# A four-layer sparse graph network: scoring one block ahead, and the order of a layer's last blocks

## The chip, the cores and the metric

The kernel runs on one core of a Trainium2 chip. The metric is the device time of one execution in microseconds (us), as a median over runs. A core has five engines that work through instruction queues of their own and wait for one another by semaphores: TensorE (PE: matrix products into the accumulation memory PSUM), VectorE (DVE: elementwise work and reductions), ScalarE (ACT: activation functions and copies), GpSimd (POOL: here it issues indirect DMAs) and SyncE (SP: here it issues plain DMAs).

## The reference, cut to what matters

The input is `x`, 4096 nodes with 256 features, and a sparse symmetric adjacency matrix `adj`. Four layers follow one another. Each normalizes the rows, clips them at zero, computes attention over each node's neighbours, and adds the result to `x`:

```
h = maximum(layernorm(x), 0);  x = x + L0(h, adj)   # 4 heads, leaky_relu 0.2, elu
h = maximum(layernorm(x), 0);  x = x + L1(h, adj)   # 1 head, leaky_relu 0.01, Wh + att @ h
h = maximum(layernorm(x), 0);  x = x + L2(adj, h)   # 4 heads, leaky_relu 0.2, biases
h = maximum(layernorm(x), 0);  x = x + L3(h, adj)   # q, k, v with 4 heads
# in each: e = score(i, j) for neighbours j;  alpha = softmax(e over j)
#          out_i = sum_j alpha_ij * value_j
```

A node's score against a neighbour is, in layers 0 to 2, a sum of two numbers, one from each node's row, and in layer 3 a product of query and key. So a layer needs, for each node, the rows of all its neighbours as the layer before left them.

## The kernel before

**Lists.** The first part (up to about 360 us in the profile) reads `adj`, finds each node's neighbours and sorts the nodes by their number of neighbours. The sorted nodes form 32 blocks of 128, one node per partition. `CAPS` gives the neighbour slots of a block: block 0 has 23 (15 of them, `KEPT`, are gathered for all its nodes, the others are shared in one more gather), then 14, 13, and so on down to 3 in block 31.

**A layer.** `layer(l)` runs layers 1 to 3 over the blocks in the order `ORDER`: 0, 30, 1, 29, 2, 28 and so on to 14, 16, 15, 31. The last five blocks are thus 17 (8 slots), 14 (9), 16 (8), 15 (8) and 31 (3); 18 (8 slots) and 13 (9) come ahead of them. `nt` is 32, `i` counts through `ORDER`, and `left` is `nt - 1 - i`. For every slot of a block, GpSimd issues one indirect DMA (`fetch`, L1048) that gathers 128 rows of the layer's table `tab[l]` in DRAM into the ring `s_ring`, 36 x 512 floats in each partition; a row has 288 floats in layer 1, 264 in layer 2 and 512 in layer 3. `fill(i)` issues the gathers of up to `AHEAD` = 4 blocks in advance, as far as ring slots are free. A layer's first gather needs every row of its table, so it waits until the layer before has written its last block.

**The steps of a block**, in layers 1 and 2:

- `scores`: VectorE and ScalarE compute the scores `e` from the gathered rows (L1554, L1565 and what follows in layer 2; in layer 1 L1550 and L1551 on ScalarE, and `mutual`, L1608 and L1612, on VectorE), the maximum (L1592, L1596), and ScalarE the exponentials (L1594, L1600).
- `weigh`, the products: VectorE makes the shares (L1626 to L1628) and multiplies the gathered rows by them in the ring (L1654), and TensorE sums the rows by products with the identity (L1662, the last one L1668) into one of three banks `s_acc`.
- `settle`: VectorE reduces the sum into `x` (L1689) and takes mean and variance (L960, L962); ScalarE works out the norm's factors in eight small instructions (L965 to L972) that `normed` issues together with the statistics.
- `norm`: ScalarE normalizes and clips (`s_h`, L975), and TensorE transposes it (L985).
- `flip`: ScalarE copies the transposed block out of PSUM (`s_ht`, L987).
- `product`: TensorE multiplies it with the next layer's weights (L1028). For layer 3 these are two products: keys and values (512 columns) and queries (256 columns).
- `third`, the row read-out: the new rows leave PSUM and go to the next layer's table. In layer 1 ScalarE copies 264 columns (L1710) and SyncE writes them (L1712). In layer 2 VectorE adds the biases, `s_kv` (L1728) and the query (L1732), SyncE writes keys and values (L1730), VectorE multiplies query and key (L1735, L1739), and ScalarE sums squares (two of L1742). `s_kv` has three buffers.

**What sets the order.** The order on PE, DVE, ACT and SP is the order in which the Python code issues instructions (`manual_schedule`); in layers 1 and 2 that holds for POOL too. `layer` keeps counters: `upto("norm", i - N)` brings the step `norm` up to the block at place `i - N`. So `S`, `N`, `F`, `Q` and `T` say how many places the steps `settle`, `norm`, `flip`, `product` and `third` stay behind; they shrink towards the layer's end. In the middle of layers 1 and 2 they are 2, 3, 4, 5 and 6. In each turn of the loop the block's scores and products stand directly behind one another:

```
            upto("norm", i - N)
            upto("product", i - Q)
            ...
            p = self.scores(l, b, self.rows[b], g)
            ...
            sums[b] = self.weigh(l, b, vs.pop(b) if l == 3 else self.rows[b][:, 0:D], g, p)
            ...
            upto("settle", i - S)
            if l < 3:
                upto("flip", i - F)
                upto("third", i - T)
```

`told_by` lets a read of PSUM wait for the last sum (L1668) of the turn in which it was written, if that turn is over. `now` is the turn's number, and `signals` holds those last sums.

Of the kernel before, what the change touches and what calls it, by code (L numbers as in the profile page):

```python
# [20 lines left out]
D = 256  # L21
# [52 lines left out]
RAW = 6  # L74

AHEAD = 4

BOUND = 4900.0


class Sparse:
# [874 lines left out]
    def normed(self, pool, xt, name):  # L956

        nc, act = self.nc, self.nc.scalar.activation
        st = pool.tile([P, 6], F32, name=f"s_st_{name}", tag="st", bufs=3)
        nc.vector.bn_stats(st, xt)  # L960
        mv = pool.tile([P, 2], F32, name=f"s_mv_{name}", tag="mv1", bufs=3)
        nc.vector.bn_aggr(mv, st)  # L962
        y = pool.tile([P, 6], F32, name=f"s_y_{name}", tag="y1", bufs=3)
        log, root, less, minus, r, at = (y[:, k : k + 1] for k in range(6))
        act(log, mv[:, 1:2], AF.Ln, bias=self.eps)  # L965
        act(less, mv[:, 1:2], AF.Identity, bias=self.minus, scale=-0.5)
        act(root, log, AF.Exp, scale=-0.5)
        act(minus, mv[:, 0:1], AF.Copy, scale=-1.0)
        act(log, root, AF.Square)
        act(less, less, AF.Identity, bias=self.three, scale=log)  # L970
        act(r, less, AF.Copy, scale=root)
        act(at, minus, AF.Copy, scale=r)  # L972
        yield None
        h = pool.tile([P, D], F32, name=f"s_h_{name}", tag="h", bufs=2)
        act(h, xt, AF.Relu, bias=at, scale=r)  # L975
        yield h
# [372 lines left out]
    def layer(self, l):  # L1349
# [89 lines left out]
        def settle(c):  # L1439
            behind[c] = self.settle(l, c, sums.pop(c), made)  # L1440
            for _ in range(2):
                next(behind[c])

        def room(k):
            if len(self.free) < k:
                upto("flip", done["norm"] - 1)
                upto("third", done["product"] - 1)
# [26 lines left out]
        def third(d):  # L1474
            if l < 3:
                step, wrote = when["row", d]
                self.reads = []
                next(rows.pop(d), None)
                if step < now:
                    for i in self.reads:  # L1480
                        told_by(i, wrote, step)
            while made and (len(made) > 1 or todo == []):
                i = self.send(*made.pop(0)).ins
                next_in_line(i)
                self.tc.declare_no_dep(i, group="results", reason="places differ")
                self.tc.add_to_no_dep_group("results", i)

        stages = {"settle": settle, "norm": norm, "flip": flip, "product": product, "third": third}
        done = {name: 0 for name in stages}

        def upto(name, k):
# [1 line left out]
                stages[name](ORDER[done[name]])  # L1493
                done[name] += 1

        for i in range(nt):
            now = i
            left = nt - 1 - i
            if l == 3:
                S = 1 if left < 3 else 2  # L1500
                N = F = Q = S + 1
                T = N
            else:
                S = 1 if left < 5 else 2
                N = 2 if left < 4 else 3
                Q = 2 if left < 2 else 3 if left < 4 else 4 if left < 6 else 5
                F, T = max(N, Q - 1), Q + 1
            fill(i)
            if (l, i) == (2, 4):
                self.symmetric()  # L1510
            b = ORDER[i]
            upto("norm", i - N)
            upto("product", i - Q)
            g = ring[:, held[b][0] : held[b][1], :]
            p = self.scores(l, b, self.rows[b], g)
            if l == 3:
                upto("third", i - T)
            sums[b] = self.weigh(l, b, vs.pop(b) if l == 3 else self.rows[b][:, 0:D], g, p)
            start, end = held.pop(b)
            past.append((start * wide, end * wide, self.read))  # L1520
            self.ever.append((start * wide, end * wide, self.read[0]))
            if l < 3:
                signals[i] = self.read[1]
            upto("settle", i - S)
            if l < 3:
                upto("flip", i - F)
                upto("third", i - T)
        now = nt
        upto("norm", nt - 2)
        upto("third", nt - 3)  # L1530
        upto("product", nt - 2)
        upto("settle", nt - 1)
        upto("norm", nt - 1)
        upto("third", nt - 2)
        upto("product", nt - 1)
        upto("third", nt - 1)

    def scores(self, l, b, mine, g):

# [48 lines left out]
        by_head = e[:, : K + 1, :].rearrange("p k h -> p h k")  # L1588
        top = pool.tile([P, H], F32, name=f"s_m_{l}_{b}", tag="m", bufs=3)
        p = self.shares[:, ts(self.turns % 2, TOPK * H)].rearrange("p (k h) -> p k h", h=H)  # L1590
        if l == 1:
            nc.vector.tensor_reduce(top, by_head, AX.X, ALU.max, negate=True)  # L1592
            tot = pool.tile([P, H], F32, name=f"s_t_{l}_{b}", tag="t", bufs=3)
# [21 lines left out]
    def weigh(self, l, b, me, g, made):  # L1615
# [12 lines left out]
        nc.vector.tensor_tensor(  # L1628
            whole(p), whole(exps), tot.unsqueeze(2).to_broadcast([P, H, K + 1]), ALU.mult
        )  # L1630
        self.turns += 1
        v0 = 0 if l < 3 else D
        acc = self.pacc.tile([P, 2, D], F32, tag="acc", name=f"s_acc_{l}_{b}")
        self.took_x[b] = nc.tensor.matmul(  # L1634
# [60 lines left out]
    def advance(self, l, b, ht, made):  # L1695
# [17 lines left out]
        else:  # L1713
# [17 lines left out]
            q = mine[:, 0:D]  # L1731
            i = nc.vector.tensor_tensor(q, ps_q, self.bqkv[:, 0:D], ALU.add)  # L1732
            self.reads.append(i.ins)
            qk = pool.tile([P, 4, 64], F32, name=f"s_qk_{b}", tag="qk", bufs=2)
            nc.vector.tensor_tensor(  # L1735
                qk, q.rearrange("p (h d) -> p h d", h=4),
# [584 lines left out]
```

## Time and profile before

| | |
|---|---|
| median of 3 runs | 1674.33 us (1669.05 to 1676.06) |
| the profiled execution's own time | 1670.3 us |
| its span in the profile | 1668.5 us |
| mean granted TensorE clock | 0.831 |
| layer 1, first gather to last | 539.5 to 875.9 us |
| layer 2, first gather to last | 902.7 to 1240.2 us |
| layer 3, first gather | 1275.2 us |

Times in a profile are microseconds from the span's start, engines are named as above (PEld is TensorE's loading of weights), and L1654 is line 1654 of the kernel before. A group's line gives the line of code, the engine and operation, what it writes and reads, the count, the busy time, the mean of one in ns, and the idle time of the engine ahead of it with what ended that. A line of the timeline gives start, duration, engine, line, operation, and in brackets the idle time ahead of it and its releaser. A line of the waits gives the waiting instruction, what it waited for, the total in us, how often, and the longest.

### The profile page before, as it was taken

The page shows a single profiled execution, that of the slowest core. Times are in us where ns is not written, and L with a number is a line of the kernel's source. Part 1 is how long each engine was busy: PE and PEld are TensorE (multiplying, and loading weights), DVE is VectorE, ACT ScalarE, POOL GpSimd, SP SyncE. Part 2 cuts the span into 40 slices and gives each one's busy share as a digit, 9 for nine tenths or more (in the row PEclk, how much of TensorE's full clock was granted, in tenths as well). Part 3 has the DMA queues.
Part 4 walks back from the last instruction along what each step waited for, and adds up shares of the span by engine and source line. Part 5 has one row for each costly group of instructions (what it writes and reads, how often), then busy time and mean ns, then how long its engine had stood idle before and what let it go on. Part 6 is the DMA issues. An engine that isn't in the chain of part 4 may idle for free.

```text
span 1668.5 us, 14028 instructions
## 1 busy us (share of the span) xinstructions
PE 1074.4 (64%) x3166; PEld 583.3 (35%) x3179; DVE 1108.8 (66%) x2651; ACT 536.1 (32%) x1754; POOL 1142.3 (68%) x1241
## 2 busy tenths in 40 slices
PE   5858888605775367787773567777793455546465
PEld 4513333203443234444442234444352232323232
DVE  5669899816885255555552456777774897888786
ACT  6966664103354033343342023333342000000000
POOL 1267777767774777777772777777753777777775
PEclk9969899857898678788897689999997677877777
DMA  7899999466552444444452445444543777767674
GB/s 267 298 395 394 365 394 331 147 222 162 155 166 69 119 120 127 132 131 134 131 137 65 108 111 148 133 139 133 142 123 106 210 220 205 213 206 211 201 209 132
DMA packets 125908, 309.07 MB, mean 185 GB/s; under 512 B 35028, under 2 KB 53463, under 8 KB 125816
## 3 DMA queue, kind: packets, MB, share of 16 engines
q0 software_dynamic: 66832, 203.64, 42.5%
q1 hardware_dynamic: 58984, 104.46, 17.8%
q8 instruction: 27, 0.44, 0.1%
q14 instruction: 65, 0.53, 0.1%
HBM read 273.00 MB, written 35.00 MB: 185 GB/s over the span
## 4 chain that ended last, share of the span: by engine, by line
POOL 25%; DVE 22%; DMA 20%; issue 15%; ACT 8%; PE 8%; DVEq 0%; POOLq 0%; ACTq 0%; SPq 0%
POOL s_ring L1048 20%; DMA s_ring<-s_tab,s_near 12%; DMA s_raw<-in_adj_dram 6%; DVE s_ring L1654 5%; POOL s_g L1048 2%; DMA s_g<-s_tab,s_keep 2%; POOL s_placed L722 2%; DVE s_ring L1575 1%; ACT s_low L277 1%; PE s_acc L1272 1%; PE s_acc L1662 1%; PE s_bank L1028 1%; DVE s_e L1579 1%; PE s_ps_t L1028 1%; POOL out_dram L1065 1%
## 5 line engine op out<-in xcount | busy, mean ns | idle before, releaser
L1048 POOL DMA_INDIRECT s_ring<-s_tab,s_near x900 | 855.9, 951 | 338.0 <-issue 264.8
L1662 PE MATMUL s_acc<-s_ring,s_ident 128*128 128x512 f32 (+1 forms) x1002 | 459.8, 616 | 275.6 <-DVE s_ring L1654 275.1
L1662 PEld LDWEIGHTS s_acc<-s_ring,s_ident 128*128 128x128 f32 x1002 | 222.2, 229 | 489.7 <-DVE s_ring L1654 305.2
L1048 POOL DMA_INDIRECT s_g<-s_tab,s_keep x192 | 182.8, 952 | 128.5 <-DMA s_raw<-in_adj_dram 66.1
L1654 DVE TENSOR_TENSOR s_ring<-s_ring,s_shares 128x2048 f32<-128x2048 f32 (+1 forms) x153 | 232.9, 1552 | 0.0
L277 ACT ACTIVATE s_low<-s_raw 128x1024 fp8e4<-128x1024 int32 x128 | 135.0, 1055 | 58.6 <-DMA s_raw<-in_adj_dram 56.8
L1600 ACT ACTIVATE s_shares<-s_e 128x40 f32<-128x40 f32 (+7 forms) x64 | 13.1, 205 | 332.7 <-DVE s_e L1597 332.7
L520 PE MATMUL s_pt<-s_low,s_mark_True 128*128 128x512 fp8e4 x256 | 83.9, 408 | 53.2 <-DVE s_cand L532 46.6
L1575 DVE TENSOR_TENSOR s_ring<-s_ring,s_shares 128x2048 f32<-128x2048 f32 (+7 forms) x47 | 78.8, 1676 | 56.4 <-DMA s_ring<-s_tab,s_near 36.4
L965 ACT ACTIVATE s_y<-s_mv,s_eps 128x1 f32<-128x1 f32 x64 | 18.8, 294 | 276.4 <-DVE s_mv L962 250.4
L532 DVE MAX8 s_cand<-s_pt 128x8 f32<-128x256 f32 x256 | 93.1, 416 | 13.8 <-PE s_pt L530 12.3
L1608 DVE TENSOR_SCALAR s_eq<-s_ring,s_own_f 128x207 bf16<-128x207 f32 (+12 forms) x32 | 12.6, 393 | 134.0 <-DMA s_ring<-s_tab,s_near 133.6
L631 PE MATMUL s_ae<-s_g,s_ident 128*128 128x512 f32 x192 | 93.0, 614 | 3.0 <-DVE s_g L622 2.9
L1579 DVE TENSOR_REDUCE s_e<-s_ring 128x32 f32<-128x2048 f32 (+7 forms) x47 | 78.9, 1679 | 1.6
L1028 PE MATMUL s_bank<-s_wkv,s_ht 128*128 128x512 f32 x128 | 63.6, 621 | 3.5 <-ACT s_ht L987 3.5
L520 PEld LDWEIGHTS <-s_mark_True 128*128 128x128 bf16 x256 | 23.6, 101 | 104.8 <-issue 61.1
L1634 PE MATMUL s_acc<-s_rx,s_ident 128*128 128x256 f32 x192 | 59.3, 392 | 0.0
L1028 PE MATMUL s_ps<-s_we_l,s_ht 128*128 128x264 f32 x128 | 43.7, 493 | 23.5 <-ACT s_ht L1310 23.5
L1668 PE MATMUL s_acc<-s_me,s_ident 128*128 128x256 f32 x192 | 57.6, 382 | 0.0
L1307 PE MATMUL s_pht<-s_ident,s_rx 128*128 128x128 f32 x64 | 14.0, 323 | 66.0 <-DMA s_ring<-s_tab,s_near 49.3
L622 DVE TENSOR_TENSOR s_g<-s_g,s_pe 128x1536 f32<-128x1536 f32 x32 | 55.4, 1735 | 0.0
L924 PE MATMUL s_bank<-s_to,s_to_row 128*128 128x32 f32 (+1 forms) x6 | 1.8, 393 | 81.8 <-DVE s_to L918 81.8
(286 smaller groups left out, 1830.8 us busy)
## 6 DMA issues: line engine op xcount, KB each, us to landing
s_raw<-in_adj_dram SPq DMA_DIRECT2D x128, 512.0 KB, 9.6
s_ring<-s_tab,s_near POOLq DMA_INDIRECT x900, 2.9
s_rx<-s_placed SPq DMA_DIRECT2D x32, 262.0 KB, 3.3
s_tab<-s_kv SPq DMA_DIRECT2D x32, 256.0 KB, 2.3
s_tab<-s_rx SPq DMA_DIRECT2D x32, 132.0 KB, 1.9
s_keep<-in_x_dram SPq DMA_DIRECT2D x8, 512.0 KB, 7.5
s_vself<-s_tab SPq DMA_DIRECT2D x32, 128.0 KB, 3.5
s_tab<-s_keep SPq DMA_DIRECT2D x7, 528.0 KB, 3.7
```

Source lines behind the costliest of these rows:

```text
L277: nc.scalar.activation(low[r][:, quarter(q)], raw.pop(q), AF.Copy, saturate=False, accum_out=self.sums[:, r, h : h + 1],)
L520: nc.tensor.matmul(pt, lhsT=self.mark[k], rhs=lo[:, k * PAIR + g * IB : k * PAIR + (g + 1) * IB], start=(k == 0), stop=False,)
L532: nc.vector.max(out=cand[:, g * (IB // CH) + k, :], in_=pt[:, ts(k, CH)])
L631: self.behind(got, nc.tensor.matmul(acc, lhsT=self.ident, rhs=g[:, :, k, 0:D], start=False, stop=(k == E - 1)))
L1028: self.writes(self.nc.tensor.matmul(ps[:, :width], lhsT=ht[:, c, :], rhs=w[:, c, :], start=(c == 0 and bias is None), stop=(c == KC - 1),))
L1048: return self.nc.gpsimd.indirect_dma_start(out=out, out_offset=None, in_=table[:, :], in_offset=bass.IndirectOffsetOnAxis(ap=idx, axis=0),)
L1575: scaled = nc.vector.tensor_tensor(kq, kq, q.unsqueeze(1).to_broadcast([P, m, D]), ALU.mult)
L1579: nc.vector.tensor_reduce(e[:, k0 : k0 + m, :], kq.rearrange("p k (h d) -> p k h d", h=4), AX.X, ALU.add)
L1634: self.took_x[b] = nc.tensor.matmul(acc[:, 1, :], lhsT=self.ident, rhs=self.x[b], start=True, stop=False)
L1654: scaled = nc.vector.tensor_tensor(v, v, p[:, k0 : k0 + m, :].unsqueeze(3).to_broadcast([P, m, H, D // H]), ALU.mult)
L1662: self.behind(self.got.get((l, b), ()), nc.tensor.matmul(acc[:, 0:n, :], lhsT=self.ident, rhs=g[:, k : k + n, v0 : v0 + D], start=False, s ...
L1668: last = nc.tensor.matmul(acc[:, 0, :], lhsT=self.ident, rhs=mev, start=False, stop=True).ins
```

## The change

Layers 1 and 2 get a new order; layer 3 has its own branch with the lags that it had. No instruction is added or taken away.

- While more than four blocks are left, the turn of block `i` first issues the scores of block `i + 1` (`score(i + 1)`), then the pending steps, and then the products of block `i`. From the last five blocks on, a block's scores are issued in its own turn.
- The lags come from a table, `LAGS`, by the number of blocks left: in the middle `settle` 2, `curve` 3, `norm` 4, `flip` 5 and `product` 6; `third` stays one behind `product`.
- ScalarE's part of a norm (L965 to L972) becomes a step of its own, `curve`, apart from the statistics on VectorE.
- `third` is cut in two for layer 2: the reads of PSUM (L1728, L1732) stay, and the rest (L1735, L1739, L1742) becomes the step `rest`. In the middle `rest` follows in the same turn; in the last five blocks it is issued no sooner than needed, three blocks later.
- In the last five blocks the read-outs are issued between a block's scores and its products. The last two turns have an order of their own.

```diff
+LAGS = [
+    (1, 1, 2, 2, 2), (1, 1, 2, 2, 2), (1, 1, 2, 2, 3), (1, 1, 3, 3, 3), (1, 2, 3, 3, 4),
+    (2, 2, 3, 3, 4), (2, 2, 4, 4, 5), (2, 3, 4, 5, 6),
+]
...
         log, root, less, minus, r, at = (y[:, k : k + 1] for k in range(6))
+        yield None
         act(log, mv[:, 1:2], AF.Ln, bias=self.eps)
...
+        def curve(c):
+            next(behind[c])
...
-                next(rows.pop(d), None)
+                upto("rest", done["third"] - 3)
+                next(rows[d], None)
...
+        def rest(d):
+            next(rows.pop(d), None)
...
+        def weigh(i):
...
+            sums[b] = self.weigh(l, b, me, block(i), scored.pop(i))
...
             if l < 3:
-                signals[i] = self.read[1]
-            upto("settle", i - S)
-            if l < 3:
+                signals[i], now = self.read[1], i + 1
...
+        for i in range(nt):
+            left = nt - 1 - i
+            fill(i)
+            if (l, i) == (2, 4):
+                self.symmetric()
+            if l == 3:
...
+            elif left > 1:
+                S, Y, N, F, Q = LAGS[min(left, len(LAGS) - 1)]
+                score(i)
+                if left > 4:
+                    score(i + 1)
+                upto("norm", i - N)
+                upto("product", i - Q)
+                upto("third", i - Q - 1)
+                if left > 4:
+                    upto("rest", i - Q - 1)
+                weigh(i)
+                upto("settle", i - S)
+                upto("curve", i - Y)
                 upto("flip", i - F)
-                upto("third", i - T)
...
+            elif left == 1:
+                upto("norm", i - 2)
+                upto("product", i - 2)
+                score(i)
+                upto("settle", i - 1)
+                upto("curve", i - 1)
+                upto("third", i - 3)
+                weigh(i)
+                upto("norm", i - 1)
+                score(i + 1)
+            else:
+                shape(i - 2)
+                upto("third", i - 3)
+                upto("settle", i - 1)
+                upto("curve", i - 1)
+                weigh(i)
+                upto("third", i - 2)
+                shape(i - 1)
+                upto("settle", i)
+                upto("curve", i)
+                upto("norm", i)
+                upto("third", i - 1)
+                shape(i)
+                upto("third", i)
+                upto("rest", i)
...
             i = nc.vector.tensor_tensor(q, ps_q, self.bqkv[:, 0:D], ALU.add)
             self.reads.append(i.ins)
+            yield
             qk = pool.tile([P, 4, 64], F32, name=f"s_qk_{b}", tag="qk", bufs=2)
```

`shape(i)` brings `norm`, `flip` and `product` up to `i`. `block(i)` is the part of the ring that holds a block.

More of the change, by code (lines that the diff above doesn't have):

```diff
@@ L1486, in third @@
                 self.tc.add_to_no_dep_group("results", i)
-        stages = {"settle": settle, "norm": norm, "flip": flip, "product": product, "third": third}
+        def rest(d):
+            next(rows.pop(d), None)
+        stages = {
+            "settle": settle, "norm": norm, "flip": flip, "product": product, "third": third,
+            "rest": rest, "curve": curve,
+        }
         done = {name: 0 for name in stages}
@@ L1494, in upto, with score @@
                 done[name] += 1
[L1496 to L1510, printed above, removed]
-            b = ORDER[i]
[L1512 to L1516, printed above, removed]
-                upto("third", i - T)
-            sums[b] = self.weigh(l, b, vs.pop(b) if l == 3 else self.rows[b][:, 0:D], g, p)
+        block = lambda i: ring[:, held[ORDER[i]][0] : held[ORDER[i]][1], :]
+        scored = {}
+        now = 0
+        def score(i):
+            b = ORDER[i]
+            if i not in scored:
+                scored[i] = self.scores(l, b, self.rows[b], block(i))
+        def weigh(i):
+            nonlocal now
+            b = ORDER[i]
+            me = vs.pop(b) if l == 3 else self.rows[b][:, 0:D]
+            sums[b] = self.weigh(l, b, me, block(i), scored.pop(i))
             start, end = held.pop(b)
@@ L1522, in layer @@
             if l < 3:
-                signals[i] = self.read[1]
-            upto("settle", i - S)
-            if l < 3:
-                upto("flip", i - F)
[L1527 to L1536, printed above, removed]
+                signals[i], now = self.read[1], i + 1
@@ new lines, in shape @@
+        def shape(i):
+            upto("norm", i)
+            upto("flip", i)
+            upto("product", i)
+        for i in range(nt):
[4 more added lines that the diff above has]
+            if l == 3:
+                S = 1 if left < 3 else 2
+                score(i)
+                upto("third", i - S - 1)
+                weigh(i)
[11 more added lines that the diff above has]
+                weigh(i)
+                upto("settle", i - S)
+                upto("curve", i - Y)
+                upto("flip", i - F)
+            elif left == 1:
+                upto("norm", i - 2)
+                upto("product", i - 2)
+                score(i)
+                upto("settle", i - 1)
[9 more added lines that the diff above has]
+                upto("curve", i - 1)
+                weigh(i)
+                upto("third", i - 2)
+                shape(i - 1)
+                upto("settle", i)
+                upto("curve", i)
+                upto("norm", i)
+                upto("third", i - 1)
+                shape(i)
+                upto("third", i)
+                upto("rest", i)
@@ L1538, in scores @@
+        if l == 3:
+            upto("third", nt - 3)
+            upto("settle", nt - 1)
+            upto("third", nt - 1)
     def scores(self, l, b, mine, g):
@@ L1590, in scores @@
         p = self.shares[:, ts(self.turns % 2, TOPK * H)].rearrange("p (k h) -> p k h", h=H)
+        self.turns += 1
         if l == 1:
@@ L1630, in weigh @@
         )
-        self.turns += 1
         v0 = 0 if l < 3 else D
```

## The prediction

> **What bounds the kernel now.** I read the page first, then GpSimd's timeline at the two borders between layers, then VectorE's waits stretch by stretch. On the page, no engine is busy for more than 68% of the span, and the chain's largest item is the row gathers at L1048:
>
> ```profile
> PE 1074.4 (64%) x3166; PEld 583.3 (35%) x3179; DVE 1108.8 (66%) x2651; ACT 536.1 (32%) x1754; POOL 1142.3 (68%) x1241
> ...
> L1048 POOL DMA_INDIRECT s_ring<-s_tab,s_near x900 | 855.9, 951 | 338.0 <-issue 264.8
> ```
>
> The timeline of GpSimd (start, duration, idle time before in brackets) shows what those 68% are. Gathers start every 1.25 us (0.95 busy, 0.30 idle), so GpSimd is full while it gathers. From the first gather of layer 1 to the first of layer 3 it pauses only twice, where a layer's first gather needs every row of the layer before:
>
> ```profile
> 874.68 0.95 POOL L1048 DMA_INDIRECT s_ring<-s_tab,s_near  x1 [0.30 <-issue]
> 875.93 0.95 POOL L1048 DMA_INDIRECT s_ring<-s_tab,s_near  x1 [0.30 <-issue]
> 902.69 0.94 POOL L1048 DMA_INDIRECT s_ring<-s_tab,s_near  x1 [25.82 <-issue]
> ...
> 1240.23 0.95 POOL L1048 DMA_INDIRECT s_ring<-s_tab,s_near  x1 [0.30 <-issue]
> 1275.22 0.94 POOL L1048 DMA_INDIRECT s_ring<-s_tab,s_near  x1 [34.05 <-PE s_bank L1767]
> ```
>
> So in layers 1 and 2 only two terms can move: the pauses of 25.82 and 34.05 us. The rest is gathers times 1.25 us, whatever VectorE does. The two layers differ in how much VectorE has to spare in their last blocks. Its waits, by cause (total us, times, longest), first in layer 1's end (820 to 880), then in the middle of layer 2 (1100 to 1200), then in its end (1200 to 1245):
>
> ```profile
> DVE s_eq L1608 <- DMA s_ring<-s_tab,s_near: 21.7, 6, 5.4
> ```
>
> ```profile
> DVE s_rx L1732 <- ACT s_ht L987: 16.6, 11, 1.6
> DVE s_e L1554 <- issue: 4.4, 3, 2.1
> DVE s_e L1554 <- DMA s_ring<-s_tab,s_near: 3.5, 2, 2.4
> ```
>
> ```profile
> DVE s_t L1626 <- ACT s_shares L1600: 2.9, 4, 1.5
> DVE s_kv L1728 <- PE s_acc L1668: 2.7, 2, 1.5
> DVE s_kv L1728 <- PE s_bank L1028: 1.6, 2, 1.0
> DVE s_rx L1732 <- ACT s_ht L987: 1.2, 2, 0.6
> ```
>
> In layer 1 VectorE waits for landings to the end: it keeps up. In layer 2's end no wait for a landing is left: it lags behind the gathers and works off what has piled up. Its timeline gives the lag:
>
> ```profile
> 1246.20 0.18 DVE L1554 TENSOR_TENSOR s_e<-s_ring,s_rx 128x32 f32<-128x32 f32 x1
> ...
> 1252.13 0.16 DVE L1554 TENSOR_TENSOR s_e<-s_ring,s_rx 128x12 f32<-128x12 f32 x1
> ...
> 1255.74 0.17 DVE L1626 TENSOR_REDUCE s_t<-s_shares 128x4 f32<-128x16 f32 x1 [2.80 <-ACT s_shares L1600]
> ```
>
> The first is the score of block 15 (8 slots, 32 elements). Its last gather is three before the last one, so issued at 1240.23 - 3 x 1.25 = 1236.5; gathers land 2.8 us after issue, so it lay ready at 1239.3 and waited 6.9 us.
>
> **Counts and queues.** The built order shows the change doing what it says, with as many instructions on every engine as before. GpSimd's and SyncE's orders are the same row for row; VectorE, ScalarE and TensorE differ in layers 1 and 2 alone. The row writes (L1712, L1730) move with the read-outs, but SyncE's queue holds them in the same order, and only the last one (issued at 1272.38, landed at 1274.37) is on the path. Layer 3 stays as it is. I cost all this at 0.
>
> **Scores one block ahead.** In the middle, VectorE's order is now score of block i+1, row read-out, products of block i. The score waits for block i+1's landing, and on VectorE the products of block i are queued behind it, then TensorE's sums, then the whole norm and product of that block. Products thus run one block of gathers later, 7 to 10 slots of 1.25 us. While GpSimd is the pace this costs nothing, because ring slots are free early: 36 x 512 / 264 = 69 slots, or 86 us from a slot's gather to its reuse. Block 18's first gather started near 1177 and its last sum ended near 1195, so 18 us are used now and some 30 then. Without that cover each step would cost up to 10 us; 50 us of it remain. What goes in the middle is the 1.62 us wait of L1732 for L987 in every step; the next thing late there is the landing itself, so this gains 0.
>
> **Layer 1's border.** The last score made ahead is that of block 17, so products enter the end one block late: 8 slots, 10.0 us. Of VectorE's waits for landings, those after that score are 5.45, 1.31 and 3.23 us (at 856.64, 865.07, 875.14), together 9.99, and 3.79 us more follow before block 31's score at 885.88. They take up the 10.0. Taken: 0. Bounds: +3.8 if the last wait can't be used, and -5.9 if VectorE's waits for ScalarE in these blocks (3.1 at L1627, 2.8 at L1565) all leave the path.
>
> **Layer 2's border.** Three terms.
> 1. Block 18 is the last that VectorE awaited (2.15 us, score at 1188.68). Its products now stand behind the score of block 13, whose last gather was issued 36 slots before the end: 1240.23 - 45.0 + 2.8 = 1198.0. So they start 9.4 us later. From there VectorE never waits for a landing, so a delay isn't won back as in layer 1: +9.4.
> 2. Row products (L1028) now trail scores by six blocks rather than five in the middle, so one more of them is left for the end. One takes from 1241.41 (transposes, L985) to 1244.44 (end of the q product, L1028), and TensorE is 88 to 100% busy from 1215 to 1245: +3.0.
> 3. In the last five blocks the rest of a row's read-out (L1735, L1739, squares at L1742) is held back three blocks, and s_kv has three buffers. L1728 of a block therefore waits for ScalarE's squares of the block three before, issued only just ahead of it and behind L987 in ScalarE's queue. Now they are long done. L987 and the squares take from 1239.57 to 1240.87, 1.3 us. The new order has VectorE's next scores or products right behind such a read at blocks 18, 13 and 14: 3 x 1.3 = +3.9.
>
> Against these stand waits that go: ScalarE's norm part now stands apart, so the exponential of block 31 needn't wait behind it (2.80 us above). With the other VectorE waits after 1205 (1.55, 1.54, 0.37, 0.72, 1.13, 0.98, 0.58, 0.27) that is 9.9 at most. I take 0 of it: most are waits for TensorE's sums and ScalarE's queue, and the held-back reads put the same kind of wait back.
>
> Sum: 9.4 + 3.0 + 3.9 = 16.3 us. As a check I laid the rows' durations out in both orders, each instruction starting when its engine and its inputs are free. The old order gives 36.8 us from the last gather to the next layer's first (the trace has 34.99), the new one 53.8: 17.0 more, an estimate from rows too. For layer 1 both orders give 27.3 (26.76 in the trace).
>
> **The clock.** TensorE's granted clock is 1.00 from 1245 to 1255, 0.83 from 1255 to 1265 and 1.00 after; its longest idle gap from 1250 to 1266 is 2.0 us. 0.83 over 10 us is 3.4 us at half clock, which costs up to 1.7 us, and a longer, emptier end may hold one to three more: +1.7 to +5.1, so 18.0 with one. I take 0 in the sum because 34.05 holds one already. [...]
>
> The profiled execution took 1670.3 us (span 1668.5, 1.8 around it), 4.0 under the median of 1674.33 and inside 1669.05 to 1676.06. It becomes 1670.3 + 16.3 = 1686.6; on the median, 1674.3 + 16.3 = 1690.6.
>
> **Rivals.**
> - Faster: VectorE's waits for ScalarE bound layer 2's end. If all 9.9 us go and the late entry is worked off by block 15's score, the time is 1674.3 - 9.9 = 1664.4. For it: 16.6 us of such waits in the middle. Against it: 10 waits in the end, none of them for a landing that could absorb the delay. It decides from the point where block 15's score starts no later than 1246.
> - No change: layer 2's end absorbs the delay as layer 1's does: 1674. It needs 16 us of slack, and VectorE is busy 7.1 to 8.9 of every 10 us from 1205 to 1255.
> - Worse: all bounds at once, three more half-clock stretches (5.1) and 3.8 in layer 1: 16.3 + 8.9 = 25.2, so 1699.5. For it: the clock of 0.83 above.
>
> **Numbers.** Forecast 0.78, worse 0.10, no change 0.06, faster 0.06. The forecast's own range runs from 16.3 - 9.9 = +6.4 (1680.7) to 1699.5; I give 1680 to 1701. A measurement of this kernel tells about 0.5% (8.4 us) from no change; slower by more than that means above 1682.7. Some 0.04 of the forecast's 0.78 falls short of that: slower 0.74 + 0.10 = 0.84, same 0.06 + 0.04 = 0.10, faster 0.06.
>
> **What would show it.** After the change GpSimd should still pause only twice: near 26 us at layer 1's border and near 50 at layer 2's (layer 2's last gather still at about 1240). Score L1554 of block 15 should start near 1262 or later, VectorE's L1732 wait of 1.62 us should be gone in the middle, and L1728 should wait for ACT L1742 in the end. A pause under 40 us, or gathers that wait for a sum in mid-layer, would prove me wrong.

## The result and the profile after

The changed kernel takes 1703.22 us (median of 4 runs, 1696.99 to 1705.9) beside 1675.01 us for the kernel before (4 runs): a ratio of 1.0174, interval 1.0154 to 1.0195. It is slower, as forecast, but by some 29 us where 16.3 were summed, and above the range's end of 1701. The profiled execution took 1704.16 us, its span is 1702.4, 33.9 more than before.

Lines have moved by about 5 ahead of the scores and by about 50 behind: the gathers are now L1053, the copy of the transposed block L992 (was L987), row products L1033 (L1028), the products L1707 (L1654), the sums L1715 and L1721 (L1662, L1668), the reads `s_kv` L1781 and query L1785 (L1728, L1732), the squares L1796 (L1742), the score of layer 2 L1607 (L1554).

The page, then GpSimd's timeline at the two borders (start, duration, idle time before):

```profile
PE 1098.0 (64%) x3166; PEld 600.3 (35%) x3179; DVE 1102.3 (65%) x2651; ACT 533.7 (31%) x1754; POOL 1143.3 (67%) x1241
...
L1053 POOL DMA_INDIRECT s_ring<-s_tab,s_near x900 | 856.2, 951 | 369.2 <-issue 283.1
```

```profile
878.34 0.95 POOL L1053 DMA_INDIRECT s_ring<-s_tab,s_near  x1 [0.30 <-issue]
914.92 0.94 POOL L1053 DMA_INDIRECT s_ring<-s_tab,s_near  x1 [35.64 <-issue]
...
1252.92 0.95 POOL L1053 DMA_INDIRECT s_ring<-s_tab,s_near  x1 [0.30 <-issue]
1309.97 1.09 POOL L1053 DMA_INDIRECT s_ring<-s_tab,s_near  x1 [56.11 <-DVE s_nm L1816]
```

The counts are unchanged and the gathers' idle time has grown from 338.0 to 369.2 us. All of that growth is in the two pauses, 25.82 to 35.64 and 34.05 to 56.11. Below, "pause" is the time from a layer's last gather to the next layer's first: 26.76 to 36.58 in layer 1, 34.99 to 57.06 in layer 2. The rest of the 33.9 is the unchanged first part, which ended 2.5 us later in this execution, and -0.5 in all else. Layer 2's gathers took 338.0 us (337.5 before): in mid-layer nothing was lost, and nothing won.

VectorE's waits in the middle of layer 2 (1100 to 1200), then in its end (1205 to 1312):

```profile
DVE s_e L1607 <- issue: 12.7, 4, 3.8
DVE s_kv L1781 <- PE s_acc L1721: 6.4, 5, 2.9
DVE s_e L1607 <- DMA s_ring<-s_tab,s_near: 4.9, 4, 1.5
```

```profile
DVE s_kv L1781 <- ACT s_sq L1796: 17.9, 5, 8.0
DVE s_kv L1781 <- PE s_acc L1721: 7.6, 4, 3.4
DVE s_kv L1781 <- PE s_bank L1033: 5.4, 3, 2.2
```

In the middle the 16.6 us of waits of the query's read for ScalarE's copy are gone, and what is late there is the score's input, the gathered rows (the third line; for the first the profile names no releaser). Waits of 6.4 us for TensorE's sums have come as well. In the end the bias reads wait 17.9 us for squares, in 5 waits; 3 of 1.3 us had been summed.

In layer 1's end, where no loss had been expected, ScalarE's waits of its copies and row read-outs were these in the kernel before (820 to 910):

```profile
ACT s_ht L987 <- PE s_bank L985: 2.3, 5, 0.8
ACT s_rx L1710 <- PE s_bank L1028: 2.1, 2, 1.1
```

In the changed kernel (840 to 915) they are:

```profile
ACT s_ht L992 <- PE s_bank L990: 12.7, 7, 4.5
ACT s_ht L992 <- PE s_acc L1721: 7.3, 2, 4.1
ACT s_rx L1763 <- PE s_bank L1033: 5.5, 3, 2.5
ACT s_rx L1763 <- PE s_acc L1721: 5.1, 2, 3.7
```

The second and the fourth line are new. The copy of a transposed block (L992) has no use for a block's sum (`s_acc`), and yet it waits for the last one, L1721. The timeline of one such wait, all engines:

```profile
860.72 0.38 PE L990 MATMUL s_bank<-s_ident,s_h 128*128 128x128 f32 x2
...
862.49 0.43 DVE L1662 TENSOR_SCALAR s_eq<-s_ring,s_own_f 128x207 bf16<-128x207 f32 x1 [0.20 <-DMA s_ring<-s_tab,s_near]
...
866.53 0.59 PE L1721 MATMUL s_acc<-s_me,s_ident 128*128 128x256 f32 x2
...
867.16 0.37 ACT L992 COPY s_ht<-s_bank 128x256 f32<-128x256 f32 x1 [4.09 <-PE s_acc L1721]
867.46 0.31 ACT L1603 ACTIVATE s_e<-s_ring,s_rx 128x9 f32<-128x9 f32 x1
...
867.99 0.17 DVE L1618 SCALAR_TENSOR_TENSOR s_e<-s_e 128x10 f32<-128x10 f32 x1 [4.67 <-ACT s_e L1604]
```

The transposes have left TensorE by 861.1 and the next block's rows have landed by 862.5, as VectorE's reading of them shows. The copy waits until 867.1 for the sum of another block. ScalarE's part of the next score (L1603, L1604) is queued behind the copy, and VectorE waits 4.67 us for that.

### The profile page after: what moved, and what is told of

Its sections match the earlier page's. It is cut to its first block, busy times and chain, and to the rows that moved or that the text cites. A ratio compares the mean times of both kernels' runs of the same rounds, so it can differ in the third digit from the quotient of the medians.

```text
span 1702.4 us, 14015 instructions
## 1 busy us (share of the span) xinstructions
PE 1098.0 (64%) x3166; PEld 600.3 (35%) x3179; DVE 1102.3 (65%) x2651; ACT 533.7 (31%) x1754; POOL 1143.3 (67%) x1241
## 4 chain that ended last, share of the span: by engine, by line
POOL 27%; DVE 20%; DMA 18%; issue 17%; PE 12%; ACT 5%; DVEq 0%; SPq 0%; POOLq 0%; ACTq 0%
POOL s_ring L1053 22%; DMA s_ring<-s_tab,s_near 9%; DMA s_raw<-in_adj_dram 6%; PE s_acc L1715 5%; DVE s_ring L1707 3%; PE s_bank L1033 2%; POOL s_g L1053 2%; DMA s_g<-s_tab,s_keep 2%; DVE s_ring L1628 2%; DVE s_e L1632 2%; POOL s_placed L726 2%; ACT s_low L281 1%; DVE s_cand L536 1%; DVE s_ring L1269 1%; PE s_ps_t L1033 1%
## 5 line engine op out<-in xcount | busy, mean ns | idle before, releaser
L1053 POOL DMA_INDIRECT s_ring<-s_tab,s_near x900 | 856.2, 951 | 369.2 <-issue 283.1
L1715 PE MATMUL s_acc<-s_ring,s_ident 128*128 128x512 f32 (+1 forms) x1002 | 449.3, 605 | 221.9 <-DVE s_ring L1707 221.9
L1715 PEld LDWEIGHTS s_acc<-s_ring,s_ident 128*128 128x128 f32 x1002 | 222.5, 228 | 427.5 <-DVE s_ring L1707 249.2
L1053 POOL DMA_INDIRECT s_g<-s_tab,s_keep x192 | 183.3, 955 | 129.1 <-DMA s_raw<-in_adj_dram 65.5
L1707 DVE TENSOR_TENSOR s_ring<-s_ring,s_shares 128x2048 f32<-128x2048 f32 (+1 forms) x153 | 233.0, 1554 | 0.0
L1654 ACT ACTIVATE s_shares<-s_e 128x40 f32<-128x40 f32 (+7 forms) x64 | 13.2, 206 | 453.5 <-DVE s_e L1651 453.5
L1662 DVE TENSOR_SCALAR s_eq<-s_ring,s_own_f 128x207 bf16<-128x207 f32 (+12 forms) x32 | 12.7, 397 | 165.5 <-DMA s_ring<-s_tab,s_near 165.4
L990 PE MATMUL s_bank<-s_ident,s_h 128*128 128x128 f32 x128 | 28.9, 317 | 96.2 <-ACT s_h L980 96.0
L1033 PE MATMUL s_bank<-s_wkv,s_ht 128*128 128x512 f32 x128 | 69.6, 672 | 4.7 <-ACT s_ht L992 2.6
L1607 DVE TENSOR_TENSOR s_e<-s_ring,s_rx 128x36 f32<-128x36 f32 (+12 forms) x32 | 6.2, 194 | 102.5 <-DMA s_ring<-s_tab,s_near 82.6
L1603 ACT ACTIVATE s_e<-s_ring,s_rx 128x9 f32<-128x9 f32 (+12 forms) x32 | 9.9, 308 | 188.4 <-DMA s_ring<-s_tab,s_near 171.3
L1687 PE MATMUL s_acc<-s_rx,s_ident 128*128 128x256 f32 x192 | 66.5, 433 | 0.0
L1033 PE MATMUL s_ps<-s_we_l,s_ht 128*128 128x264 f32 x128 | 44.2, 498 | 24.0 <-ACT s_ht L1315 24.0
L1721 PE MATMUL s_acc<-s_me,s_ident 128*128 128x256 f32 x192 | 58.6, 387 | 0.0
L990 PEld LDWEIGHTS s_bank<-s_ident,s_h 128*128 128x128 f32 x128 | 15.6, 152 | 114.2 <-ACT s_h L980 112.0
```

The lines of the kernel that those rows point to most:

```text
L1033: self.writes(self.nc.tensor.matmul(ps[:, :width], lhsT=ht[:, c, :], rhs=w[:, c, :], start=(c == 0 and bias is None), stop=(c == KC - 1),))
L1053: return self.nc.gpsimd.indirect_dma_start(out=out, out_offset=None, in_=table[:, :], in_offset=bass.IndirectOffsetOnAxis(ap=idx, axis=0),)
L1687: self.took_x[b] = nc.tensor.matmul(acc[:, 1, :], lhsT=self.ident, rhs=self.x[b], start=True, stop=False)
L1707: scaled = nc.vector.tensor_tensor(v, v, p[:, k0 : k0 + m, :].unsqueeze(3).to_broadcast([P, m, H, D // H]), ALU.mult)
L1715: self.behind(self.got.get((l, b), ()), nc.tensor.matmul(acc[:, 0:n, :], lhsT=self.ident, rhs=g[:, k : k + n, v0 : v0 + D], start=False, s ...
L1721: last = nc.tensor.matmul(acc[:, 0, :], lhsT=self.ident, rhs=mev, start=False, stop=True).ins
```

## The experiments

The source of that wait is one line of the diff, `signals[i], now = self.read[1], i + 1`. Before, a turn's number `now` stood still through the turn, so a copy issued in the turn of its transposes waited for them directly. Now `now` is moved on as soon as the products are issued. A copy behind them counts as one of a past turn, and `told_by` hangs it on their last sum. By the table of lags that concerns the turns with six, five, four and two blocks left, in which `flip` takes up, behind the products, a block whose `norm` was issued ahead of them.

So three theories were set against one another: **late entry** (products one block late, not won back), **queued waits** (that copy, and the squares in ScalarE's queue), and **half clock** (TensorE's granted clock). All times:

| run | what it is | ratio to before (95%) | pause, layer 1 | pause, layer 2 |
|---|---|---|---|---|
| before | | 1 | 26.76 | 34.99 |
| after | the change | 1.0174 (1.0154 to 1.0195) | 36.58 | 57.06 |
| e1 | change, no score ahead | 1.0081 (1.0064 to 1.0098) | 27.84 | 46.11 |
| e2 | change, reads wait for their own data | 1.0115 (1.0095 to 1.0135) | 26.23 | 54.54 |
| e3 | change, rest of read-outs at once | 1.0160 (1.0136 to 1.0184) | 31.88 | 56.03 |
| e4 | change, middle lags as before | 1.0155 (1.0138 to 1.0172) | 34.82 | 52.71 |
| e5 | e1 to e4 together | 0.9999 (0.9983 to 1.0015) | 24.68 | 37.97 |
| e6 | e5 with the score ahead | 1.0068 (1.0043 to 1.0094) | 27.04 | 47.88 |
| e7 | before with the score ahead | 1.0094 (1.0067 to 1.0121) | 33.29 | 45.10 |
| e8 | change with more TensorE work | 1.0174 (1.0148 to 1.0200) | 32.78 | 60.32 |
| e9 | layer 1 of e5, layer 2 of before | 0.9958 (0.9944 to 0.9972) | 24.57 | 35.99 |
| e10 | e6, score ahead ended 12 turns earlier | 0.9992 (0.9979 to 1.0005) | 24.71 | 38.52 |
| e11 | before with such a wait added | 1.0046 (1.0029 to 1.0062) | 30.69 | 39.55 |
| e12 | e5, products six places behind | 1.0009 (0.9996 to 1.0022) | 25.95 | 38.53 |

The median of before was between 1671.5 and 1675.0 us in these comparisons, so ratios are compared, not times. The pauses come from one profile each. How far that carries is shown by kernels with the same instructions in the same order on every engine: in layer 1 the pauses of after and e3 lie 4.7 us apart, those of e5 and e9 0.1; in layer 2 those of after and e8 lie 3.3 apart, those of before and e9 1.0. So a difference of less than some 3 to 5 us is not settled by one pair of pauses, and the ratios, good to 2 to 4.5 us, settle no finer.

### e1: no score ahead

```diff
-                if left > 4:
-                    score(i + 1)
```

> Only the score of block i + 1 ahead of the products of block i is taken back; the rest of the change stays. Three theories. Late entry (the products enter each layer's end one block late and none of it is won back): layer 1's pause of GpSimd falls from 36.6 us to 24 to 27, layer 2's from 57.1 to about 47, the time from 1703 to about 1680. Queued waits (ScalarE's copy of a transposed block waits for the sums of the block just multiplied, and VectorE's bias reads wait for squares queued behind that copy): both waits are still there, the pauses fall by 2 us at most, 1700. Half clock (TensorE at half clock for 27 us of the 92 us from 820 to 912): the time falls only as far as the half-clock stretches in the two ends do, 1692 if layer 1's are gone.

Measured: 1685.03 us (1682.37 to 1685.92), 0.9% of the change's 1.74% gone, pauses 8.7 and 11.0 us shorter. That is late entry's forecast for layer 2. In layer 1 the pause is back too, although the copy's new wait is still in the code, so the next run was needed to say whose it is.

### e2: the copy waits for its own data

```diff
-                if step < now:
+                if step < turn:
...
-            left = nt - 1 - i
+            turn, left = i, nt - 1 - i
```

> A read of PSUM whose data were written in the same turn waits for that write alone, as in the kernel before, and no longer for the last sum of the block that was multiplied in between; the rest of the change stays. Queued waits: ScalarE's waits for the last sum in layer 1's end (7.3 us at the copy of the transposed block) go, VectorE's scores behind them come earlier, layer 1's pause falls by 4 to 7 us to about 31, layer 2's by 1 to 2, the time from 1703 to about 1697. Late entry: another wait takes their place, 1702. Half clock: no change beyond what the half-clock stretches do, 1698 to 1706.

The same line is changed at the row read-outs. Measured: 1690.87 us (1686.3 to 1692.68). Layer 1's pause falls by 10.3 us, to 0.5 under the kernel before, with the score ahead still in place. Part of that may be the clock: from 820 to 905 TensorE's granted clock was 0.82 in after and 0.88 in e2. It was 0.88 in e3 too, whose layer 1 is the change's own, and from e3 to e2 the pause falls by 5.6 us. ScalarE's waits in layer 1's end (840 to 906):

```profile
ACT s_ht L992 <- PE s_bank L990: 9.3, 8, 2.4
ACT s_rx L1763 <- PE s_bank L1033: 4.7, 3, 2.6
ACT s_rx L1763 <- PE s_acc L1721: 3.7, 1, 3.7
```

The copy's wait for L1721 is gone and none took its place; VectorE's waits for the score's term fall from 13.7 to 7.3 us. So layer 1's loss needs both causes: without the score ahead (e1) or without the wait (e2) it isn't there. Queued waits had forecast a fall of 4 to 7 us for layer 1, late entry none; it fell by 5.6 to 10.3.

### e11: the wait alone, in the kernel before

```diff
+        done_to = 0
...
-                if step < now:
+                if step < max(now, done_to):
...
-                signals[i] = self.read[1]
+                signals[i], done_to = self.read[1], i + 1
```

> The kernel before with one part alone: a read of PSUM issued behind the products of its own turn waits for their last sum even if its data were written ahead of them (in the last six turns, where the copy of the transposed block follows in the turn of the transposes). If the wait costs by itself, layer 1's pause rises by 2 to 4 us and layer 2's by 4 to 6, the time from 1674 to 1680 to 1684. If it costs only behind a late entry, both pauses stay within 2 us and the time within 0.2% of before.

Measured: 1681.42 us (1678.49 to 1683.1), pauses 3.9 and 4.6 us longer. The wait costs by itself, as the first alternative had it, also where nothing enters late. Its trace shows the way in layer 1's end (820 to 910), first ScalarE's waits, then VectorE's for ScalarE's score term, in e11 and then in the kernel before:

```profile
ACT s_rx L1711 <- PE s_acc L1669: 2.7, 1, 2.7
...
ACT s_ht L987 <- PE s_acc L1669: 1.0, 1, 1.0
```

```profile
DVE s_e L1566 <- ACT s_e L1552: 10.3, 5, 6.6
```

```profile
DVE s_e L1565 <- ACT s_e L1551: 6.6, 5, 3.8
```

ScalarE's reads wait 3.7 us for the last sum (L1669 here), and VectorE's waits for ScalarE grow by as much. But 2.7 of the 3.7 us are a row read-out (L1711). In the order of the kernel before, read-outs stand behind a turn's products, and the change issues them ahead. So e11 shows that a wait of this kind costs time, and not what the copy's wait costs alone.

### e7: the score ahead alone, in the kernel before

```diff
+        scored = {}
...
-            p = self.scores(l, b, self.rows[b], g)
+            for j in (i, i + 1) if l < 3 and left > 4 else (i,):
+                c = ORDER[j]
+                if j not in scored:
+                    view = ring[:, held[c][0] : held[c][1], :]
+                    scored[j] = self.scores(l, c, self.rows[c], view)
+            p = scored.pop(i)
...
```

> The kernel before with one part of the change alone: the score of block i + 1 ahead of the products of block i while more than four blocks are left; lags, read-outs and norms as before. The working ahead of the result took this part at 0 in layer 1 and 9.4 us in layer 2: 1674 + 9.4 = 1683. If layer 1 does not absorb it either (8 slots, up to 10 us), its pause rises from 26.8 to 33 or more, layer 2's from 35 to 45 to 47, and the time to 1688 to 1692.

Measured: 1688.87 us (1686.28 to 1691.33), pauses 6.5 and 10.1 us longer. Layer 2 gives the term of 9.4. Layer 1 does not absorb the late entry here, although the copy's new wait isn't in this kernel. VectorE's waits there (820 to 910):

```profile
DVE s_e L1571 <- ACT s_e L1557: 17.2, 5, 6.8
DVE s_eq L1615 <- DMA s_ring<-s_tab,s_near: 13.9, 4, 4.9
```

The waits for landings shrank from 21.7 to 13.9 us, as the prediction had it, but the waits for ScalarE's term of the score grew from 6.6 to 17.2. In this order, that of the kernel before, ScalarE's norm part is issued with the statistics and waits for VectorE's (29.8 us in 8 waits from 820 to 913; 30.2 in 7 in the kernel before), and the score's term is queued behind. With the change's own order of norms and read-outs (e2, e6) VectorE's wait for the score's term is 7.3 and 7.2 us, and the pause is that of the kernel before. That the place of the norm's part is what decides was not isolated.

### e3: the rest of the read-outs at once

```diff
+                upto("rest", done["third"])
...
-                if left > 4:
-                    upto("rest", i - Q - 1)
+                upto("rest", i - Q - 1)
```

> The rest of a row's read-out in layer 2 (query times key, squares) is issued right behind its two reads in the last five blocks as well; the rest of the change stays. Queued waits: VectorE's 17.9 us of waits for ScalarE's squares in layer 2's end go; if all of it is on the path, layer 2's pause falls from 57 to about 40 and the time to 1686. Late entry: the waits move to TensorE's products and sums, the pause falls by 2 to 4 us, 1700. Layer 1 is not touched: its pause stays at 36 within what the clock moves it.

Measured: 1697.91 us (1693.39 to 1702.06), layer 2's pause 1.0 us shorter. The waits in layer 2's end (1205 to 1304), to be held against the second list of after above:

```profile
DVE s_kv L1781 <- PE s_acc L1721: 17.5, 8, 3.5
DVE s_kv L1781 <- PE s_bank L1033: 9.0, 5, 3.8
```

The 17.9 us for squares are gone to the last tenth, and waits for TensorE's sums and products have taken their place: 7.6 to 17.5, 5.4 to 9.0. The reads stood in the same queue as before and something else was nearly as late. Taking away 17.9 us of waits shortened the pause by 1.0 us, which one pair of profiles can't tell from nothing; the forecast of 17 is excluded.

### e4 and e12: the trail of six places

e4 puts the middle lags back to what they were, the norm's two parts together and the row products five places behind. e12 takes e5 and moves the products alone:

```diff
-    (2, 2, 3, 3, 4), (2, 2, 4, 4, 5), (2, 3, 4, 5, 6),
+    (2, 2, 3, 3, 4), (2, 2, 4, 4, 5), (2, 2, 3, 4, 5),
```

```diff
-    (2, 2, 3, 3, 4), (2, 2, 4, 4, 5), (2, 2, 3, 4, 5),
+    (2, 2, 3, 3, 4), (2, 2, 4, 4, 5), (2, 2, 3, 4, 6),
```

> Rows are made five places behind the scores in the middle of a layer, as before, rather than six; the rest of the change stays. If one more row product left for the end costs what was summed for it, layer 2's pause falls by 3 us and the time from 1703 to 1700; layer 1, whose products are a third as long, by under 1 us. Under the theories of late entry, queued waits and half clock alike it is the small term: if the time falls below 1697, the trail of six places costs more than one product.

> e5 with one number changed: row products six places behind the scores in the middle of a layer, as in the change, rather than five; settle, norm's parts and copies as in e5. If one more product left for the end costs what was summed for it, layer 2's pause rises by 3.0 us from e5's 38.0 to 41 and the time from 1672.7 to 1676. If it is hidden (the extra product is made in the turn before the last six, beside VectorE's work) the pause stays within 1 us of 38, and what e4 won back (4.4 us of pause) was the norm's part standing apart, which delays each block's transposes by one place.

Measured: e4 1698.0 us (1694.31 to 1698.59), layer 2's pause 4.4 us shorter than in the change; e12 1673.92 us (1672.17 to 1678.72), the pause 0.6 longer than in e5. So the second forecast of e12 came: one more product left for the end is hidden. The table of lags shows where: `product` goes from 6 to 5 places behind when six blocks are left, so that turn makes two. By subtraction 3.8 us of e4's 4.4 would belong to the norm part standing apart with everything behind it one place later. That is an estimate: the two pairs differ in whether the score is ahead, both numbers are of the size that one profile leaves open, and no run has the norm part apart alone.

### e5, e6 and e10: late entry by itself

e5 joins e1 to e4. e6 is e5 with the score ahead, e10 is e6 with

```diff
-                if left > 4:
+                if left > 16:
                     score(i + 1)
```

> All four undone parts together: no score ahead, reads as in e2, rest as in e3, trail as in e4. What is left of the change is ScalarE's norm part apart and the order of the last two turns, with read-outs between scores and products. If the four prices add up (15.7, 9.8, 2.8 and 2.7 us on the times of e1 to e4), 1703 - 31 = 1672, equal to the kernel before within 0.5%. Late entry and queued waits overlap in layer 1 (each of e1 and e2 alone brought its pause to 26 to 28): if the shared part is counted once, layer 1's pause is 22 to 26, layer 2's 38 to 42, the time 1668 to 1676. If something else of the change costs time that none of the four touches, layer 2's pause stays above 43 and the time above 1680.

> As e5, but with the score ahead kept. Its difference from e5 is the price of late entry by itself, with the queued waits gone: laid out from rows of before it is 4 us in layer 1 and 10 in layer 2, so 14 us over e5, near 1684. If the score ahead costs only through the queued waits, e6 is as e5 within 3 us.

> e6 with the score ahead only while more than 16 blocks are left, so that it ends ten turns before VectorE's last wait for a landing in layer 2 and not at it. If a late entry is won back wherever VectorE still waits for landings (7.9 us in the 100 us of layer 2's middle before, so some 8 in ten turns), layer 2's pause falls from e6's 47.9 us to 38 to 40, layer 1's to 24 to 26, the time from 1685 to about 1675. If the delay is carried whatever the place where the score ahead stops, layer 2's pause stays at 46 or more and the time at 1685.

Measured: e5 1672.73 us (1671.24 to 1677.64), e6 1685.14 us (1682.86 to 1686.19), e10 1672.06 us (1669.28 to 1674.35). In layer 2 the four parts take away 11.0 + 2.5 + 1.0 + 4.4 = 18.9 us singly and 19.1 together: there they add up, as far as one profile each tells. In layer 1 they overlap, as e1 and e2 had shown. e6 over e5 is late entry by itself: 2.4 us in layer 1, 9.9 in layer 2. And e10 shows why the 9.9 is not won back: with the score ahead ended 12 turns earlier, ten turns ahead of VectorE's last wait for a landing, the same delay is won back whole, 38.5 us beside e5's 38.0.

### e9: the version that the runs point to

Layer 1 in the order of e5, layer 2 in that of the kernel before:

```diff
+            elif l == 2:
+                S = 1 if left < 5 else 2
+                N = 2 if left < 4 else 3
...
+                score(i)
+                weigh(i)
+                upto("settle", i - S)
+                upto("curve", i - S)
+                upto("flip", i - F)
+                upto("third", i - T)
             elif left > 1:
...
```

> The version that the runs so far point to: layer 1 in the order of e5 (pause 24.7 us against 26.8 before), layer 2 in the order of the kernel before (35.0 against 38.0 in e5). If the 3.0 us that e5 keeps in layer 2 lie in the order of its last turns, layer 2's pause is 35 again, the sum 2 us under the kernel before, 1672 on a median of 1674; if they come from the clock or the run, layer 2's pause stays at 37 to 38 and the time at 1675.

Measured: 1668.07 us (1665.45 to 1670.05) beside 1672.95, a ratio of 0.9958 (0.9944 to 0.9972; the two medians alone give 0.9971): a little faster than both kernels. Its pauses:

```profile
877.36 0.94 POOL L1053 DMA_INDIRECT s_ring<-s_tab,s_near  x1 [0.30 <-issue]
901.93 0.95 POOL L1053 DMA_INDIRECT s_ring<-s_tab,s_near  x1 [23.63 <-issue]
...
1239.15 0.94 POOL L1053 DMA_INDIRECT s_ring<-s_tab,s_near  x1 [0.30 <-issue]
1275.14 0.94 POOL L1053 DMA_INDIRECT s_ring<-s_tab,s_near  x1 [35.05 <-PE s_bank L1843]
```

Layer 1's pause is 2.2 us shorter than before, layer 2's 1.0 longer, so 1.2 us of the gain are seen in the profiles. The medians differ by 4.9; the profile of before is one of its faster executions, 4.0 under its median of then. Of the 3.0 us that e5 keeps in layer 2, 2.0 would lie in its order of read-outs and last turns; before and e9 themselves, with the same order there, differ by 1.0.

### e8: TensorE kept from idling

```diff
+        for _ in range(3 if self.warm else 0):
+            self.writes(nc.tensor.matmul(
+                pt[:, : KC * P], lhsT=self.ident, rhs=self.we2[:, 0, : KC * P],
+                start=True, stop=True,
+            ))
...
+            self.warm = l == 1 and left < 12
```

> The change with three products more (128 x 256, into the bank that the transposes overwrite) ahead of each transpose in layer 1's last 12 turns, some 1.3 us of TensorE's work each at full clock, so that TensorE is not idle while it waits for ScalarE's normalized block. Half clock: the half-clock stretches from 820 to the last gather (27 us from 820 to 912 in the profile of after) fall by half or more, and layer 1's pause falls from 32 to 37 us to 30 or less though 16 us of work is added. Late entry or queued waits: TensorE's added work is on the path, the pause rises by 6 to 9 us to 40 or more. Layer 2 is not touched.

Measured: 1703.85 us (1700.28 to 1704.85), the change's own ratio. The table by stage, of after and then of e8; a row ends with the granted clock, the DMA engines' share and GB/s, and begins with the busy times of TensorE, its weight loads, VectorE, ScalarE and GpSimd:

```profile
820.00:880.00 60.00, 53.00 (x146) 31.80 (x146) 30.03 (x67) 25.53 (x104) 44.97 (x48) 0.81 0.52 137
880.00:916.00 36.00, 26.94 (x90) 16.90 (x89) 13.23 (x36) 14.60 (x57) 0.94 (x1) 0.84 0.09 30
```

```profile
820.00:880.00 60.00, 55.10 (x193) 35.88 (x194) 31.88 (x69) 27.93 (x115) 45.37 (x49) 0.94 0.51 139
880.00:916.00 36.00, 29.56 (x120) 20.71 (x118) 14.10 (x36) 14.49 (x57) 3.55 (x4) 0.95 0.14 42
```

The granted clock rose from 0.81 and 0.84 to 0.94 and 0.95, so the products kept it up, as half clock had forecast. The pause of 32.78 lies inside what the change's layer 1 shows in other executions (31.88 in e3, whose layer 1 is the same, to 36.58), and neither forecast for it, 30 or less nor 40 or more, came. So no gain beyond the cost of the added work is seen. Layer 2, which e8 doesn't touch, came out 3.3 us longer than in after, at nearly the same granted clock (0.90 and 0.91 from 1205 to 1312). The cause of layer 1's loss is the wait and the late entry that e2 and e1 take away; that the clock makes it larger or smaller by a few us is likely, and not shown by a run. After and e3 differ by 4.7 us of pause in layer 1 with the same instructions there, at granted clocks of 0.82 and 0.88.

## Why the prediction was wrong, step by step

- **Two pauses, nothing else.** Right. Gathers in mid-layer took the same time, and the ring's room covered the later products.
- **The middle.** Right: the 1.62 us wait went, the landing came in its place, at no gain.
- **Layer 1's border, taken 0 with bounds of -5.9 to +3.8. This step failed**: +9.8 in the profile of after, +5.1 in that of e3, whose layer 1 is the same. The working set the 10.0 us of late entry against VectorE's waits for landings. What it missed is a wait that the change adds on ScalarE, in a line of the diff that the prediction doesn't mention. The copy of the transposed block waits for the sums of the block multiplied in between, and the next block's score is queued behind the copy. Late entry brings that sum onto the path: there the wait is worth 10.3 us (after to e2), or 5.6 at the same granted clock (e3 to e2). Without it the change's border is where the prediction had it: e2 gives 26.2 us, e6 27.0, beside 26.76 before. That is in part luck. e6 is 2.4 above e5, so as far as one profile tells the late entry is not quite absorbed, and the rest of the new order makes about as much good. In the order of the kernel before, from whose rows the prediction worked, the delay costs 6.5 us (e7), for a reason that was not isolated.
- **Layer 2, late products: +9.4.** Right: 9.9 (e6 to e5), 10.1 (e7 to before), 11.0 (e1). The reason given, that VectorE never waits for a landing from there on, is what e10 shows.
- **Layer 2, one more row product: +3.0.** Not seen: 0.6 (e12). The product was counted into the end, where TensorE is full (88 to 100% busy from 1215 to 1245 in before), but it is made in the turn with six blocks left, ahead of it.
- **Layer 2, reads that wait for squares: 3 x 1.3 = +3.9.** The wait was foreseen and came, larger than sized: 17.9 us, because the squares are queued behind a copy that itself waits for TensorE. Its longest, first on ScalarE, then on VectorE:

```profile
1277.44 0.37 ACT L992 COPY s_ht<-s_bank 128x256 f32<-128x256 f32 x1 [4.90 <-PE s_bank L1033]
```

```profile
1278.80 0.69 DVE L1781 TENSOR_TENSOR s_kv<-s_bank,s_bqkv 128x512 f32<-128x512 f32 x1 [8.04 <-ACT s_sq L1796]
```

Its price was 1.0 (e3), because TensorE's sums were nearly as late: without the wait for squares, 7.6 us of waits for them became 17.5.
- **Layer 2, not in the sum at all**: the copy's wait, 2.5 (e2); the norm's part standing apart, some 3.8; the order of read-outs and last turns, some 2.0. With 9.9 + 0.6 + 1.0 that makes 19.8 of the 22.1 us. Only the 9.9 is clear of what one profile leaves open. For the rest the total is known better than its parts: beside late entry layer 2 lost some 12 us where 6.9 were summed, and how they divide stays open. So the 16.3, near the 22.1 as it looks, held two terms of which the runs show little and lacked others.
- **Waits that go, taken 0.** Right, on the cautious side: VectorE's 6.2 us of waits for the exponential in layer 2's end (1190 to 1275) are gone in after, and the time didn't fall. The rival called all 9.9 us waits for ScalarE; three of them (1.54, 1.13 and 0.98) are waits for TensorE in the trace.
- **The check by laid-out durations** agreed with the sum, 17.0 and 16.3, and both were too low; for layer 1 it gave no change. As it is described, an instruction in it starts when its engine and its inputs are free, and a copy held for a sum that it doesn't read is not in that. It worked from the same rows as the sum, so it was no second witness. Which of its steps failed in layer 2 stays open.
- **Signs to look for.** Two pauses, the end of the 1.62 us wait and the squares' wait came as said. Block 15's score began at 1281.52, 28.6 us after layer 2's last gather, where some 22 were forecast (6.0 before). The sign that failed is "near 26" in layer 1, with 35.64; for that and for the later start of layer 1 the last gather of layer 2 came at 1252.92 and not at 1240. "Near 50" in layer 2 came as 56.11.

## What to carry to other kernels

In a kernel whose order is written by hand, go through every changed counter as well as every moved instruction: a counter that decides what a read waits for is a new wait, and it is priced by what is queued behind it. Work ahead on an engine that keeps the issued order is late entry for what stands behind it; here it was free as long as that engine still waited for landings in the turns that followed (layer 2's pause is 38.5 us in e10, 47.9 in e6 and 38.0 without the score ahead, in e5), so end it well ahead of the last such wait. And run the same order twice before a difference of a few us is given a cause. A wait's total in a profile is not its price: ask what else was due at the same moment (here 17.9 us of waits went, and the pause was 1.0 us shorter).

## What the runs showed of the hardware

TensorE falls to half clock several times in layer 1's end; the longest of its idle gaps from 820 to 905 in after is 2.60 us. Its timeline there, and the row by stage from 840 to 850, whose third number from the end is the granted clock:

```profile
836.41 0.59 PE L1721 MATMUL s_acc<-s_me,s_ident 128*128 128x256 f32 x2
839.14 0.44 PE L990 MATMUL s_bank<-s_ident,s_h 128*128 128x128 f32 x2 [2.13 <-ACT s_h L980]
...
842.61 1.24 PE L1029 MATMUL s_bank<-s_be_l,s_line 1*128 1x264 f32 x2
843.78 2.13 PE L1033 MATMUL s_bank<-s_we_l,s_ht 128*128 128x264 f32 x4
```

```profile
840.00:850.00 10.00, 10.00 (x20) 5.59 (x19) 5.40 (x12) 5.96 (x25) 7.56 (x9) 0.50 0.54 144
```

A gap of 2.13 us is followed by 10 us at half clock (0.50) with TensorE busy throughout; a row product's four parts take 2.13 us there and 1.16 at full clock (at 853.27, granted clock 1.00). The half-clock stretches of this end last 3.4, 6.8 or 10.2 us. A gap's length alone doesn't tell: ahead of the stretches from 829.4, 839.7 and 870.4 TensorE was busy for 0.98, 1.28 and 1.14 of 3.41 us (the length of the shortest stretch), with gaps of 2.60, 2.13 and 2.27, but ahead of the one from 890.9 for 2.45, with a gap of 0.96 us; and 3.42 us with 1.99 busy (904.52 to 907.94) brought none. What decides is not shown. The prediction had priced such stretches at up to 1.7 us each and taken 0; in layer 1 two executions of the same order differ by 4.7 us of pause, at granted clocks of 0.82 and 0.88 from 820 to 905.
